# The first product of a four-layer graph network kernel: one plain slice, then three slices by seven products

## The chip, the cores and the metric

The kernel runs on one core of a Trainium2 chip. The metric is the device time of one execution in microseconds, as the median of several runs; lower is better. Everything is computed in fp32.

## What is computed

`x` holds 8 batches of 2048 nodes with 64 features, `adj` is a dense 2048 x 2048 matrix. Four layers follow each other, each of the form `x = layernorm(x + layer(x))`. The change touches layer 0 only:

```
# layer 0, K = 3: As = [I, A, 2 A A - I]
x_g = einsum('knm,bmc->bnkc', A_stack, x)        # x, A x, 2 A (A x) - x
w   = einsum('nd,dkio->nkio', embedding, weight)  # weights of each node
b   = einsum('nd,do->no', embedding, bias)
x   = layernorm(x + einsum('bnki,nkio->bno', x_g, w) + b)
```

Layer 1 has two products with A in a row, each followed by weights and a relu; layer 2 has one; layer 3 has two, for A x and 2 A (A x) - x. Their weights are 64 x 64 for all nodes.

## The kernel before

`x` is laid out as 16 tiles of 128 nodes by 512 columns (8 batches of 64), kept on chip in `xy`, which has two slots for each node tile: slot 0 is x, slot 1 takes a product. A product with `adj` is a 2048 x 2048 by 2048 x 512 multiplication. TensorE holds a 128 x 128 piece of x (two batches, one "pair" p of four) as stationary operand and streams a piece of `adj` past it, up to 512 columns. One source matmul in fp32 is two matmul instructions in the trace.

**The later products** (`product`, lines 189 to 330) use a scheme of seven multiplications in place of eight, at two levels: `adj` is cut into quarters, sums of quarters stand in `comb[q]` in HBM, and sums of x are formed on VectorE. The names of the seven at the outer level are A11, A12, A22, S1, S2, S3 and S4; at the inner level (`inner`, line 207), seven of eight blocks again, each sub-sum being an addition of 128 x 512.

**The first product** (lines 545 to 597, matmuls at L558) doesn't use the scheme, as the sums aren't there yet: it multiplies plainly and, while doing so, VectorE forms the sums of `adj` that the later products load. It runs over four slices `ns`; slice `ns` holds the node tiles ns, ns + 4, ns + 8, ns + 12 of the output, all inputs, as four chunks `j` of 1 MB (L146). The chunks live in a ring of four buffers, so chunk j of the next slice can only be loaded when TensorE and VectorE are done with chunk j of this one. A slice is 4 chunks x 4 pairs x 4 tiles = 64 source matmuls of 512 columns.

For each slice `prepare` (L465) makes on VectorE: the inner sums of A11, A12 and A22 (tag `C`, four buffers of 1 MB), and S1, S2, S4, S3 (tag `T`, three buffers of 1 MB), each with inner sums of its own. Every one is written to `comb` by DMAs that GpSimd issues (L478): 10 MB a slice. GpSimd's queue is in order, and so is SyncE's, which issues the loads.

At the end of a slice ACT copies the four PSUM banks to `hT` (L581; tags u2 and u3, one buffer each), a DMA writes `hT` to `t1T` in HBM, and a job `back` is queued that transposes `hT` back to nodes (L336, L337) into slot 1. Jobs wait in `pump`, which runs one step of one job after each group of four matmuls. `biases` (L539), 16 small matmuls, is such a job. In the last slice VectorE adds the biases `pb` to slot 0 and centres it (L573 to L576), one chunk after another.

`load_weights` is called after slice 0; its loads stand in SyncE's queue ahead of the chunks of slice 1. `sum_weights` turns the weights into the forms that are used, in slice 1.

The tile framework orders instructions for each engine; an instruction in `keep_in_program_order` isn't moved against others. After the first product, `product(1, ...)` starts with the inner products A11 and S1, before the feature work of layer 0 (L633 to L652), which adds onto slot 0.

Of the kernel before, what the change touches and what calls it, by code (L numbers as in the profile page):

```python
# [16 lines left out]
P = 128  # L17
# [75 lines left out]
def kernel(  # L93
# [311 lines left out]

    if True:
        l0 = first.enter_context(tc.tile_pool(name="l0", bufs=1))
        e_sb = l0.tile([P, NT, D], F32, tag="e_sb", name="e_sb")
        nc.gpsimd.dma_start(e_sb, emb)

        wn = l0.tile([P, 3, D, F], F32, tag="wn", name="wn")

        def center(w, half=slice(0, P)):
            shape = list(w.shape)
            m = small.tile([P, shape[1]], F32, tag="wm", name="wm")[half]
            nc.vector.tensor_reduce(m, w, AX.X, ALU.add)
            nc.vector.scalar_tensor_tensor(
                w, m.unsqueeze(2).to_broadcast(shape), -1.0 / F, w, ALU.mult, ALU.add
            )

        def load_weights():
            for k in range(2):
                nc.sync.dma_start(wn[k * F : (k + 1) * F], w_l0.rearrange("n i d o -> i n d o"))
            nc.gpsimd.memset(wd, 0.0)
            w3 = l0.tile([P, 5, F], F32, tag="s", name="w3", bufs=2)
            for k in range(2):
                half = slice(k * F, (k + 1) * F)
                for i, src in ((W1A, w_l1[0]), (W1B, w_l1[1]), (W2N, w_neigh), (W2S, w_self)):
                    nc.sync.dma_start(wd[half, i, half], src)
                nc.sync.dma_start(w3[half], w_l3.rearrange("(k i) o -> i k o", i=F))  # L430
            nc.sync.dma_start(b2, b_l2.to_broadcast([P, F]))
            nc.sync.dma_start(b3, b_l3.to_broadcast([P, F]))
            return w3

        def sum_weights(w3):
            nc.vector.tensor_tensor(wn[:, 0], wn[:, 0], wn[:, 2], ALU.subtract)
            nc.vector.tensor_scalar(wn[:, 2], wn[:, 2], 2.0, None, ALU.mult)

            for k in range(2):
                half = slice(k * F, (k + 1) * F)  # L440
                nc.vector.tensor_tensor(wd[half, W3A, half], w3[half, 1], w3[half, 3], ALU.add)
                nc.vector.tensor_tensor(w3[half, 2], w3[half, 2], w3[half, 4], ALU.add)
                nc.vector.tensor_tensor(wd[half, W3X, half], w3[half, 0], w3[half, 2], ALU.subtract)
                nc.vector.tensor_scalar(wd[half, W3AA, half], w3[half, 2], 2.0, None, ALU.mult)


            for k in range(2):
                half = slice(k * F, (k + 1) * F)
                center(wd[half, W2N:, half], half)
            for w in (W2S, W3X):  # L450
                nc.vector.tensor_tensor(wd[:, w, :], wd[:, w, :], ident, ALU.add)
            center(wn.rearrange("p n d o -> p (n d) o"))
            for k in range(2):
                half = slice(k * F, (k + 1) * F)
                for n, w in enumerate((W3A, W3X)):
                    nc.vector.tensor_copy(w3o[half, n], wd[half, w, half])
                for n, w in enumerate((W2N, W2S)):
                    nc.vector.tensor_copy(w2o[half, n], wd[half, w, half])
            center(b2.unsqueeze(1))
            center(b3.unsqueeze(1))  # L460

        def prepare(ns, ch):

            ch = [c.rearrange("p m i n -> p i m n") for c in ch]

            def add(out, a, b, op=ALU.add):
                nc.vector.tensor_tensor(out, a, b, op)

            def kept(tag, shape, bufs):
                s = sums.tile([P, *shape, GW], F32, tag=tag, name="s" + ("i" if tag == "C" else "o"), bufs=bufs)
# [25 lines left out]
            def rq(I, J):  # L498
                return lambda c: ch[2 * J + c][:, 2 * I : 2 * I + 2]
# [4 lines left out]
            def put(q, s):  # L504
# [2 lines left out]
                keep(q, 3, flat[:, 3:])  # L507
                inner(q, *(flat[:, k].rearrange("p (m n) -> p m n", m=TG) for k in range(4)))

            inner(A11, *raw(0, 0))  # L510
            inner(A12, *raw(0, 1))
            inner(A22, *raw(1, 1))
            s1 = outer(rq(1, 0), rq(1, 1), ALU.add)
            put(S1, s1)
            s2 = outer(sq(s1), rq(0, 0), ALU.subtract)
            put(S2, s2)
            s4 = outer(rq(0, 1), sq(s2), ALU.subtract)
            put(S4, s4)
            s3 = outer(rq(0, 0), rq(1, 0), ALU.subtract)
            put(S3, s3)  # L520

        with tc.tile_pool(name="p_n", bufs=4, space=PSUM) as p_n, tc.tile_pool(
            name="p_tn", bufs=2, space=PSUM
        ) as p_tn, tc.tile_pool(name="p_b", bufs=1, space=PSUM) as p_b:

            rise = p_tn.tile([P, TG, P], F32, tag="pt", name="rise")
            for k in range(8):
                nc.tensor.matmul(rise[:, k % TG, :], ident, ident, start=True, stop=True)

            bias0 = sums.tile([D, F], F32, tag="p1", name="bias0")  # L530
            nc.scalar.dma_start(bias0, b_l0)
            pb = p_b.tile([P, NT, F], F32, tag="pb", name="pb")
            eT = [l0.tile([D, GW], F32, tag="xT" if g < 2 else "tT", name="eT", bufs=2) for g in range(NG)]
            for g in range(NG):
                nc.scalar.dma_start(eT[g], embT[:, ts(g, GW)])

            def biases():
                for t in range(NT):
                    tc.keep_in_program_order(nc.tensor.matmul(  # L539
                        pb[:, t, :], eT[t // TG][:, ts(t % TG, P)], bias0, start=True, stop=True  # L540
                    ))
                    if t % TG == TG - 1:
                        yield

            for ns in range(TG):
                tiles = slice(ns, NT, TG)
                ps = [p_n.tile([P, GW], F32, tag="mm", name="ps_n") for p in range(NP)]
                ch = [chunks.pop((ns, j)) for j in range(NG)]
                prepare(ns, ch)
                if ns == 1:  # L550
                    sum_weights(w3)
                for j in range(NG):
                    steps = [(p, m) for p in range(NP) for m in range(TG)]
                    if ns == 0 and j == 0:

                        steps = [(p, m) for m in range(TG) for p in range(NP)]
                    for k, (p, m) in enumerate(steps):
# [5 lines left out]
                            stop=(j == NG - 1 and m == TG - 1),  # L563
                            skip_group_check=True,
                        )
                        if ns == j == k == 0:
                            tc.keep_in_program_order(mm)
                        if k % TG == TG - 1:
                            pump.step()
                    if ns == TG - 1:  # L570
                        v = xy[:, j * TG : (j + 1) * TG, 0, :].rearrange("p t (b f) -> p t b f", f=F)
                        bias = pb[:, j * TG : (j + 1) * TG, :].unsqueeze(2).to_broadcast([P, TG, B, F])
                        nc.vector.tensor_tensor(v, v, bias, ALU.add)  # L573
                        sm = small.tile([P, TG, B], F32, tag="xm", name="xm")
                        nc.vector.tensor_reduce(sm, v, AX.X, ALU.add)
                        nc.vector.scalar_tensor_tensor(  # L576
                            v, sm.unsqueeze(3).to_broadcast([P, TG, B, F]), -1.0 / F, v, ALU.mult, ALU.add
                        )
                for p in range(NP):
                    hT = sums.tile([P, GW], F32, tag=f"u{2 + p % 2}", name="hT")  # L580
                    nc.scalar.copy(hT, ps[p])  # L581
                    nc.sync.dma_start(
                        t1T[p].rearrange("f (i n c) -> f i n c", i=NG, n=TG)[:, :, ns],
                        hT.rearrange("f (i c) -> f i c", i=NG),
                    )

                    def back(p=p, hT=hT, tiles=tiles):
                        to_nodes(1, p_tn, tiles, p, hT)
                        yield
                    pump.add(back())  # L590
                if ns + 1 < TG:
                    for j in range(NG):
                        chunks[ns + 1, j] = slice_chunk(ns + 1, j)
                if ns == 0:
                    w3 = load_weights()
                    pump.add(biases())
            pump.drain()

        p_mm = ctx.enter_context(tc.tile_pool(name="p_mm", bufs=2, space=PSUM))
        if True:  # L600
            p_y = first.enter_context(tc.tile_pool(name="p_y", bufs=3, space=PSUM))


            order = [
# [5 lines left out]
            def fetch(k):  # L610
                if k < len(order):
                    i, p = order[k]
                    fetched[i, p] = [l0.tile([P, GW], F32, tag=n, name=n, bufs=2) for n in ("xT", "tT")]
                    for tile_, src in zip(fetched[i, p], (xT, t1T)):
                        nc.sync.dma_start(tile_, src[p][:, ts(i, GW)])

            def feature0(g, p, hT):
# [4 lines left out]
                for k in range(TG):  # L622
# [1 line left out]
                    acc = xy[:, t, 0, ts(p, 2 * F)].rearrange("p (b f) -> p b f", f=F)  # L624


                    s = l0.tile([P, DH, 2, F], F32, tag="s", name="s", bufs=2)
                    for h in range(2):
                        y = p_y.tile([P, 2, DH * F], F32, tag="y", name="y")
                        for n in range(3):  # L630
# [159 lines left out]
```

## Time and profile before

| | us |
|---|---|
| median of 3 runs (1723.04 to 1724.67) | 1723.25 |
| the profiled execution | 1724.72 |
| its span | 1722.9 |
| mean granted TensorE clock | 0.997 |
| first product: first matmul at | 6.05 |
| first product: end of its last matmuls at | 241.0 |

The busy shares of the engines in stretches of the first 250 us (us busy; the last two columns are the mean busy share of the 16 DMA engines and what they moved):

| stretch, us | TensorE | VectorE | ACT | DMA share | GB/s |
|---|---|---|---|---|---|
| 0 to 25 | 22.52 | 5.20 | 1.28 | 0.92 | 327 |
| 25 to 50 | 25.00 | 20.55 | 0.00 | 1.02 | 338 |
| 50 to 75 | 22.91 | 20.00 | 2.25 | 1.02 | 386 |
| 75 to 100 | 25.00 | 21.06 | 2.24 | 0.79 | 274 |
| 100 to 125 | 25.00 | 5.76 | 1.17 | 0.92 | 359 |
| 200 to 225 | 25.00 | 22.14 | 0.41 | 1.01 | 375 |

A busy share says how long an engine had something to do, not whether that was on the path that sets the end. The chain that ended last goes back from the last instruction through what released each one; its pieces, in order of time, show how long a run of instructions took from start to start. In a row of instructions the columns are line, engine, operation, output and inputs, shapes and count, busy time and mean duration in ns, and the idle time in front of it with what ended it. In a row of the windows they are the stretch, its length, busy us (and instructions) of TensorE, its weight loads, VectorE, ACT and GpSimd, the granted clock, the DMA share and GB/s.

### The profile page before, as it was taken

The numbers are of one execution on the slowest core, as the hardware profiler recorded it, in microseconds if no ns is written. First come the engines' busy times: TensorE is split into PE (matmuls) and PEld (weight loads), VectorE is DVE, ScalarE is ACT, GpSimd is POOL, SyncE is SP. The second block draws the span as 40 slices with busy tenths as digits, with TensorE's granted clock in tenths as the row PEclk, the third lists the DMA queues.
The fourth block names the chain that finished last, engine by engine and source line by source line (L and its number), as shares of the span: only waits on it lengthen the run. The fifth ranks groups of instructions, "written<-read, shape, count | busy, mean of one in ns | idle before, by whom it ended". The sixth has DMA issues, their size and how long they took to land.

```text
span 1722.9 us, 15569 instructions
## 1 busy us (share of the span) xinstructions
PE 1704.1 (99%) x5664; PEld 798.5 (46%) x5664; DVE 921.2 (53%) x1650; ACT 271.4 (16%) x772; POOL 258.5 (15%) x332
## 2 busy tenths in 40 slices
PE   9999999999999999999999999999999999999997
PEld 4444444444444444444455455554444455554443
DVE  4845773546546655544443264873557434443556
ACT  0100110232233333330001010221001012100001
POOL 1212200345245445441000000000000000000000
PEclk9999999999999999999999999999999999999999
DMA  9888768424422222227877877667888866678893
GB/s 325 331 324 317 253 233 302 149 86 138 167 86 99 86 99 86 98 74 291 314 273 268 296 279 250 221 221 258 294 294 285 302 229 214 225 263 301 316 314 123
DMA packets 82235, 391.19 MB, mean 227 GB/s; under 512 B 8848, under 2 KB 25232, under 8 KB 42608
## 3 DMA queue, kind: packets, MB, share of 16 engines
q1 hardware_dynamic: 70176, 346.94, 57.0%
q0 software_dynamic: 11248, 42.08, 6.7%
q10 hardware_dynamic: 736, 1.18, 0.2%
q8 instruction: 45, 0.74, 0.2%
q14 instruction: 30, 0.25, 0.0%
HBM read 339.84 MB, written 50.33 MB: 226 GB/s over the span
## 4 chain that ended last, share of the span: by engine, by line
PE 95%; DVE 3%; DMA 1%; ACT 0%; POOL 0%; issue 0%; POOLq 0%; ACTq 0%
PE mmb L225 25%; PE y L633 19%; PE mmc L225 16%; PE mma L225 16%; PE ps_n L558 12%; PE z L681 2%; PE z L711 2%; DMA t1T<-hT 1%; PE pt L672 1%; PE pt L727 1%; DVE ss L368 0%; PE pt_n L336 0%; DVE sm L352 0%; DVE xy L353 0%; DVE xy L378 0%; PE pb L539 0%
## 5 line engine op out<-in xcount | busy, mean ns | idle before, releaser
L225 PE MATMUL mmb<-a,t 128*128 128x512 f32 x1008 | 456.6, 595 | 0.0
L225 PEld LDWEIGHTS mmb<-a,t 128*128 128x128 f32 x1008 | 187.1, 190 | 227.2 <-issue 222.9
L641 DVE SCALAR_TENSOR_TENSOR xy<-y,e_sb,xy 128x128 f32<-128x128 f32 x512 | 179.7, 351 | 122.3 <-PE y L633 106.3
L558 PE MATMUL ps_n<-a,xy 128*128 128x512 f32 x512 | 225.5, 598 | 2.1 <-ACT hT L581 2.1
L650 POOL TENSOR_TENSOR s<-s 128x512 f32<-128x512 f32 (+2 forms) x192 | 167.0, 870 | 349.9 <-ACT s L645 339.9
L645 ACT ACTIVATE s<-y,e_sb 128x128 f32<-128x128 f32 x512 | 139.2, 383 | 293.1 <-PE y L633 293.1
L225 PE MATMUL mma<-a,T 128*128 128x512 f32 x384 | 173.5, 594 | 1.7 <-ACT p L240 1.7
L198 DVE TENSOR_TENSOR u<-mmb,p 128x512 f32<-128x512 f32 x84 | 58.0, 691 | 198.9 <-PE mmb L225 198.7
L225 PE MATMUL mmc<-a,t 128*128 128x512 f32 x336 | 152.4, 595 | 0.0
L558 PEld LDWEIGHTS ps_n<-a,xy 128*128 128x128 f32 x512 | 96.9, 192 | 118.5 <-issue 115.7
L633 PE MATMUL y<-wn,xT 64*128 64x512 f32 x512 | 135.6, 602 | 0.0
L633 PE MATMUL y<-wn,tT 64*128 64x512 f32 x512 | 132.1, 589 | 0.0
L225 PE MATMUL mma<-a,xy 128*128 128x512 f32 x288 | 130.5, 595 | 0.8 <-ACT hT L581 0.8
L633 PE MATMUL y<-wn,C 64*128 64x512 f32 x512 | 131.3, 589 | 0.0
L225 PEld LDWEIGHTS mma<-a,T 128*128 128x128 f32 x384 | 71.0, 190 | 87.1 <-issue 84.2
L198 DVE TENSOR_TENSOR C<-mmc,C 128x512 f32<-128x512 f32 x60 | 41.4, 690 | 109.5 <-PE mmc L225 109.5
L225 PEld LDWEIGHTS mmc<-a,t 128*128 128x128 f32 x336 | 61.5, 190 | 71.4 <-issue 71.0
L225 PE MATMUL mmc<-a,T 128*128 128x512 f32 x192 | 86.5, 593 | 0.0
L225 PEld LDWEIGHTS mma<-a,xy 128*128 128x128 f32 x288 | 53.5, 190 | 65.3 <-issue 61.2
L633 PEld LDWEIGHTS y<-wn,xT 64*128 64x128 f32 x512 | 47.1, 186 | 70.2 <-issue 70.2
L240 ACT COPY p<-mma 128x512 f32<-128x512 f32 x42 | 24.6, 586 | 343.3 <-PE mma L225 343.3
L633 PEld LDWEIGHTS y<-wn,tT 64*128 64x128 f32 x512 | 49.9, 187 | 60.3 <-issue 60.3
(97 smaller groups left out, 1340.7 us busy)
## 6 DMA issues: line engine op xcount, KB each, us to landing
a<-comb SPq DMA_DIRECT2D x240, 1024.0 KB, 4.8
a<-in_blocks SPq DMA_DIRECT2D x54, 1024.0 KB, 4.9
comb<-si POOLq DMA_DIRECT2D x28, 1024.0 KB, 10.0
a<-in_slices SPq DMA_DIRECT2D x15, 1024.0 KB, 9.8
comb<-so POOLq DMA_DIRECT2D x16, 512.0 KB, 11.4
comb<-so POOLq DMA_DIRECT2D x16, 256.0 KB, 11.8
t1T<-hT SPq DMA_DIRECT2D x16, 256.0 KB, 4.0
xT<-in_xT SPq DMA_DIRECT2D x16, 256.0 KB, 3.0
```

The lines of the kernel that those rows point to most:

```text
L198: nc.vector.tensor_tensor(out, a, b, op)
L225: nc.tensor.matmul(ps, xb[:, m, :], a[:, :, m, :], start=(start and m == 0), stop=(m == TG - 1), skip_group_check=True,)
L240: nc.scalar.copy(p1, pa)
L558: mm = nc.tensor.matmul(ps[p], xcol(0, TG * j + m, p), ch[j][:, m], start=(j == 0 and m == 0), stop=(j == NG - 1 and m == TG - 1), skip_gr ...
L633: nc.tensor.matmul(y[:, b, :], terms[n][half, ts(k, P)], wn[half, n, h * DH : (h + 1) * DH, :], start=(n == 0), stop=(n == 2),)
L641: nc.vector.scalar_tensor_tensor(acc, y[:, :, ts(d, F)], e, acc, ALU.mult, ALU.add)
L645: nc.scalar.activation(s[:, d], y[:, :, ts(d, F)], AF.Copy, scale=e)
L650: nc.gpsimd.tensor_tensor(s[:, :n], s[:, :n], s[:, n : 2 * n], ALU.add)
L672: nc.tensor.transpose(pt[:, ts(k, P)], xy[:, g * TG + k, slot, ts(p, 2 * F)], ident)
L681: nc.tensor.matmul(z[:, k, :], aT[:, ts(k, P)], wd[:, w, :], start=(n == 0), stop=(n == len(terms) - 1),)
L711: nc.tensor.matmul(z[n][:, k], xT[half, ts(k, P)], w[half], start=True, stop=True)
L727: nc.tensor.transpose(pt[:, k, :], hT[:, ts(k, P)], ident)
```

## The change

Slice 0 stays plain. Slices 1 to 3 use the scheme of seven at one level: S1 to S4 and the raw quarters of `adj` are streamed as they are made for `comb` (they lie on chip anyway), 256 columns at a time, past sums of x. Those sums, T1 to T4, are formed once on VectorE during slice 0; two of them lie in tiles of slot 1 that are written last (so slice 2's `back` jobs are held until slice 3 has used T1), two in a new pool `xs`. A slice becomes 7 products x 16 source matmuls of 256 columns. `prepare` is a generator now and forms the sums in another order, pinned from slice 1 on. Results are joined on VectorE (`plus`, `done`) rather than copied by ACT. `hT` has five buffers (tag `t`, which also takes `w3`); `w3` is loaded by ACT's queue. The biases are added in four pieces (`join_bias`), and centring is put into jobs that `product(1, ...)` runs during its first two inner products.

```diff
         def load_weights():
...
-            w3 = l0.tile([P, 5, F], F32, tag="s", name="w3", bufs=2)
+            w3 = sums.tile([P, 5, F], F32, tag="t", name="w3", bufs=5)
...
-                nc.sync.dma_start(w3[half], w_l3.rearrange("(k i) o -> i k o", i=F))
+                nc.scalar.dma_start(w3[half], w_l3.rearrange("(k i) o -> i k o", i=F))
...
-            inner(A11, *raw(0, 0))
-            inner(A12, *raw(0, 1))
-            inner(A22, *raw(1, 1))
-            s1 = outer(rq(1, 0), rq(1, 1), ALU.add)
-            put(S1, s1)
-            s2 = outer(sq(s1), rq(0, 0), ALU.subtract)
-            put(S2, s2)
-            s4 = outer(rq(0, 1), sq(s2), ALU.subtract)
-            put(S4, s4)
-            s3 = outer(rq(0, 0), rq(1, 0), ALU.subtract)
-            put(S3, s3)
+            outers[S1] = s1 = outer(rq(1, 0), rq(1, 1), ALU.add)
+            outers[S2] = s2 = outer(sq(s1), rq(0, 0), ALU.subtract)
+            inner(A11, *raw(0, 0))
+            outers[S3] = s3 = outer(rq(0, 0), rq(1, 0), ALU.subtract)
+            yield
+            put(S1, s1)
+            yield
+            put(S2, s2)
+            outers[S4] = s4 = outer(rq(0, 1), sq(s2), ALU.subtract)
+            inner(A12, *raw(0, 1))
+            inner(A22, *raw(1, 1))
+            yield
+            put(S3, s3)
+            put(S4, s4)
+            yield
...
+            def sums_of_x():
+                sub = ALU.subtract
+                nc.vector.tensor_tensor(T[0], xq(0, 1), xq(0, 0), sub)
+                nc.vector.tensor_tensor(T[1], xq(1, 1), T[0], sub)
+                nc.vector.tensor_tensor(T[2], xq(1, 1), xq(0, 1), sub)
+                nc.vector.tensor_tensor(T[3], xq(1, 0), T[1], sub)
...
+                def mul(ps, a, b, start=True):
+
+                    for p in range(2):
+                        for k in range(NT // 2):
+                            nc.tensor.matmul(
+                                ps[:, ts(p, GW // 2)], b(k, p), a(k // TG, k % TG),
+                                start=(start and p == k == 0), stop=(k == NT // 2 - 1),
+                                skip_group_check=True,
+                            )
+                        pump.step()
+                    return ps
...
+                next(parts)
+                pa = mul(bank(), raw(0, 0), x_of(0, 0))
+                p1 = sums.tile([P, GW], F32, tag="p1", name="p1")
+                nc.scalar.copy(p1, pa)
+                load_chunks(ns + 1, 0, 1)
+                next(parts)
+                p2 = mul(bank(), raw(0, 1), x_of(1, 0))
+                if ns == TG - 1:
+                    join_bias(0, 1)
+                    join_bias(0, 0)
+                pc = mul(bank(), summed(S1), t_of(1))
+                for job in held:
+                    pump.add(back(*job))
+                next(parts)
+                if ns == 1:
+                    sum_weights(w3)
+                elif ns == 2:
+                    sum_wn()
+                pb_ = mul(bank(), summed(S2), t_of(2))
+                u2 = plus("u2", pb_, p1)
+                done(0, p2, p1)
+                pd = mul(bank(), raw(1, 1), t_of(4))
+                load_chunks(ns + 1, 2, 3)
+                nc.vector.tensor_tensor(u2, pc, u2, ALU.add)
+                next(parts)
+                if ns == TG - 1:
+                    join_bias(1, 0)
+                mul(pb_, summed(S3), t_of(3), start=False)
+                u3 = plus("u3", pb_, p1)
+                done(3, pc, u3)
+                done(2, pd, u3)
+                pe = mul(bank(), summed(S4), x_of(1, 1))
+                done(1, pe, u2)
+                return [hT[p] for p in range(NP)]
...
+        def centered(h, c):
...
+            tc.keep_in_program_order(nc.vector.tensor_reduce(sm, v, AX.X, ALU.add))
+            yield
...
+                nc.vector.scalar_tensor_tensor(v, sm, -1.0 / F, v, ALU.mult, ALU.add)
+            )
+            yield
+
+        for h, c in ((0, 0), (0, 1), (1, 1), (1, 0)):
+            pump.add(centered(h, c))
```

`sum_wn` is the part of `sum_weights` that treats `wn`, in slice 2 now. `outer` writes a whole quarter sum, `put` writes it to `comb` and forms its inner sums, `done` adds a product half to a joined part into `hT`.

## Prediction

> **What bounds the kernel now.** I read the page's engine row first, then the chain that ended last, then the chain piece by piece for the first 250 us, which is all that the change touches.
>
> ```profile
> PE 1704.1 (99%) x5664; PEld 798.5 (46%) x5664; DVE 921.2 (53%) x1650; ACT 271.4 (16%) x772; POOL 258.5 (15%) x332
> ...
> PE 95%; DVE 3%; DMA 1%; ACT 0%; POOL 0%; issue 0%; POOLq 0%; ACTq 0%
> ...
> L558 PE MATMUL ps_n<-a,xy 128*128 128x512 f32 x512 | 225.5, 598 | 2.1 <-ACT hT L581 2.1
> ```
>
> TensorE is the chain: 95% of the span, and L558, the first product, is some 219 us of it. It idled there for 2.1 us in all, so time goes only if TensorE's stream shortens and nothing new makes it wait. A source matmul is two instructions in the trace (512 for 256 written).
>
> The pieces of the chain give the price of one instruction:
>
> ```profile
> 143.09 44.63 PE ps_n L558 x104
> ```
>
> 44.63 / 104 = 0.429 us for 512 columns; the mean of 598 ns in the group includes overlapped latency and isn't used. For narrow ones, TensorE's timeline in a later stage:
>
> ```profile
> 1002.35 1.05 PE L681 MATMUL z<-wd,C 128*128 128x128 f32 x8
> 1003.24 3.60 PE L225 MATMUL mmc<-a,t 128*128 128x512 f32 x8
> ```
>
> Eight instructions of 128 columns, each with its own weights, take 1003.24 - 1002.35 = 0.89 us, 0.111 us each. And the one stall, on the same timeline:
>
> ```profile
> 69.09 0.60 PE L336 MATMUL pt_n<-ident,hT 128*128 128x128 f32 x4
> 71.79 5.40 PE L558 MATMUL ps_n<-a,xy 128*128 128x512 f32 x8 [2.09 <-ACT hT L581]
> 77.02 0.60 PE L336 MATMUL pt_n<-ident,hT 128*128 128x128 f32 x4
> ```
>
> After 2.09 us of idling, eight instructions took 5.40 us against 3.43. The windows show why, and what the DMA engines did meanwhile:
>
> ```profile
> 60.00:64.00 4.00, 4.00 (x11) 1.77 (x10) 3.87 (x11) 0.00 (x0) 0.00 (x0) 1.00 1.01 416
> ...
> 72.00:76.00 4.00, 4.00 (x6) 1.62 (x6) 4.00 (x6) 1.23 (x3) 0.00 (x0) 0.57 0.99 336
> ...
> 80.00:84.00 4.00, 4.00 (x14) 2.00 (x13) 4.00 (x7) 0.59 (x1) 1.14 (x2) 1.00 0.08 30
> ```
>
> The granted clock (third from the end) fell to 0.57. The DMA share (next) is 1.0 in nearly every such window from 4 to 76 us: the first slice is DMA-bound in bytes although TensorE doesn't feel it. The waits name the stall's cause: hT has one buffer per tag and its previous copy to t1T was slow.
>
> ```profile
> ACT hT L581 <- DMA t1T<-hT: 18.2, 2, 15.4
> ```
>
> **Part by part.**
>
> *Matmuls.* Slices 1 to 3 held 384 instructions of 512 columns: 384 x 0.429 = 164.8 us. They become 3 x 7 products x 16 x 2 = 672 of 256 columns. No row has 256 columns; a line through 128 (0.111) and 512 (0.429) gives 0.217, so 672 x 0.217 = 145.9. Saved 18.9 us. Bounds: half of a 512 is 0.2146 (144.2 us, 1.7 more saved), 10 ns more each would cost 6.7. A rule of the Trainium skill speaks against the change (TensorE: Matmul & The Clock Gate, "Measured speedup vs the span model"): a weight load overlaps a running matmul only when it goes to another row group. Here all are 128 x 128, and this trace's weight loads last 190 ns. If they were exposed, an instruction would cost 0.213 + 0.190 = 0.403, 271 us, 106 us slower. But z's 0.111 us per instruction is shorter than one 190 ns load, so loads do overlap here; the row decides. Bias matmuls (4 x 1.03 us) and transposes (0.44 per four) keep their number.
>
> *hT buffers.* hT moves to five buffers of tag t, so ACT doesn't wait for t1T after slice 0. The stall goes: 2.1 idle plus 5.4 - 3.4 = 2.0 of slow clock, 4.1 us. The skill's advice (same page, "Why this matters for your kernels") is to avoid idling beyond about 3 us; by it a 2.09 us stall costs only itself. This row shows twice that, and I use the row. Next to be late there is slice 1's chunk 3, below.
>
> *VectorE.* Per fast slice: 28 inner additions at 0.60 spacing (17), 8 outer halves of 1.14 to 1.22 (9.5), u2, u3 and the second u2 addition (2.1), 8 half evictions, costed by the 128x256 addition from z at L716 (0.416, 3.3): 32 us, plus 8.6 for wn in slice 2 or 6.9 for three join_bias in slice 3, of some 50 us of TensorE. The order is pinned, so I laid both queues side by side. In slice 2, from its start: done(1) of slice 1 until 1, S1's sums 3.5, S2's 5.9, A11 and S3's 10.9, inner sums of S1 and S2 and done(0) 16.6; s4 waits for the third product, 22.5 (its buffer is S1's); A12 and A22 until 29.8; u2 at 33, needed by the accumulating S3 product at 36.2; u3 45.2, done(3) 46, needed at 50.2 by the next slice. All hide with 3 to 4 us in hand. Behind s4's wait stand A12, A22 and u2; u2 has the thinnest margin, 1 to 3 us in slice 1. Sums of x (4 x 2.28 = 9.1) fall into slice 0, where VectorE was busy 5.2 of the first 25 us: nothing, as slice 1 first needs them at 80.
>
> *Chunks.* Chunks 0 and 1 of the next slice can load once S3's sum and the first product are over, some 11 us into a slice, and have over 30 us. Chunks 2 and 3 load after the fifth product (36 us in), needed 21 us later; landing took 8.9 us in the median, 17.0 at most. Hidden, except in slice 1: there chunk 3 needs the buffer that slice 0 uses to its end, and the fast slice reads it in its second product.
>
> ```profile
> 61.98 0.33 SPq L146 DMA_DIRECT2D a<-in_slices  x1
> ```
>
> ```profile
> 79.01 1.29 DVE L469 TENSOR_TENSOR si<-a 128x512 f32<-128x512 f32 x2 [2.93 <-DMA a<-in_slices]
> ```
>
> The first row is SP's timeline, the second VectorE's. In before it was issued at 61.98 and was there at 79.0, behind three other chunks issued at 48 to 51 and the t1T writes. Slice 0 ends at 62.0, so TensorE needs it at 62.0 + 2 x 3.47 + two bias groups of 1.03 + half a group, 1.7, = 72.7. SP's queue is the weights, then chunks 0, 1, 2, three t1T writes, then chunk 3. Without two w3 loads in it, and with S3's sum early on VectorE, chunks 0 and 1 go at some 41 instead of 48; chunk 2 at some 55 (VectorE waits in slice 0 for S1's write to free s4's buffer). From 48 to 79 this queue moved about 5 MB, 155 GB/s, beside the saturated writes. From 55.5: chunk 2, 0.75 MB of t1T, chunk 3, 2.75 MB / 155 GB/s = 17.7, so 73.2. Wait 0.5 us; the bounds are 0 and 79.0 - 72.7 = 6.3 plus 2 of slow clock. I take 2.5, nearer to the queue sum than to before's landing, with some for the clock and u2.
>
> *w3* moves to ACT's queue behind the hT copies: issued about 62, landing in 9.2 (median before), so 71 to 72, and slice 1's weight sums stand on VectorE between the halves of S1's sum. S1's product is at 80, the sum at 75 to 77: nothing, up to 3 if w3 takes 15.
>
> *Biases and end of stage.* Three join_bias (2.29 each) hide as above; the last follows the stage's end, 2.3 us before the new product's first difference. Until now bias and reduction (4.6) stood there. The first two transposes no longer wait for ACT's hT copies (0.8 idle). Together nothing, -1 to +1.
>
> *Deferred centring.* Eight operations of 2.29 = 18.3 us enter the first two inner products of product 1 (16 groups of 3.43 = 55 us), where VectorE is busy some 20 now by its timeline. A u addition must come within one group (3.43) after its product; one centring operation plus the addition is 3.0. The long differences (2.28) added once make 0.3. I take 0.4, 0 to 4; without cover, 18.3. From product 1's feature work onward every engine's order is unchanged.
>
> **Sum.** 18.9 + 4.1 - 2.5 - 0.4 = 20.1 us. The profiled run is 1724.7 (span 1722.9, 1.8 around it), giving 1704.6; it lies 1.5 over the median of 1723.25, so the median to expect is 1703.2, say 1703.5.
>
> **Rivals.**
> - *Chunk 3 of slice 1 as late as before.* It speaks for this that the DMA engines are full until 76 us in any order, and that the sums of slice 0 end some us later. Then 8.5 instead of 2.5: 1709.5. Against it: SP's queue drains earlier.
> - *Writes of sums hold VectorE in slices 2 and 3.* 15 MB per slice in 50 us is 300 GB/s; saturated windows moved 340 to 420. If C buffers come free late, VectorE slips past its 3 to 4 us of margin, 3 to 5 us per slice with slow clock: about 1713.
> - *Slower: exposed weight loads.* Place: each of 672 instructions. Gain and loss balance at (164.8 + 4.1 - 2.9) / 672 = 0.247 us, so from 34 of the 190 ns exposed. With 48 exposed, 0.261 x 672 = 175.4: 10.6 lost, 4.1 won, 2.9 of waits, so 1733. Against it: z at 0.111.
> - *That it doesn't do what it says* is excluded: the built order has 336 source matmuls of 256 columns (672 instructions) and 64 of 512.
>
> **Numbers.** Forecast 72% (its own range 1700 to 1707), late chunk 15%, writes 7%, exposed loads 3%, other losses 3%. Low end 1700: no waits and 0.2146 per instruction would be 1698.7, which needs all at once. High end 1710.5 takes in the late chunk. A difference under about 0.2% (3.4 us) can't be told from none. Faster 0.94, same 0.02, slower 0.04.
>
> **What would show it.** 256-column instructions at 0.214 to 0.22 spacing in the chain; no clock loss near 70 us, or a short wait for in_slices at about 72 at the first fast slice's second product; the stage ending near 221 instead of 241; product 1's first 55 us with VectorE full but TensorE at 4.00 of 4.00. I am wrong if the spacing is over 0.23, if waits recur in slices 2 and 3, or if u additions wait for centring.

## The result, and the profile after

The changed kernel takes 1704.0 us (median of 4 runs, 1703.34 to 1711.45) beside 1723.96 for the kernel before on the same chip (4 runs, 1723.04 to 1725.07): a ratio of 0.9894, 95% interval 0.9866 to 0.9922. The profiled execution took 1703.86 us, its span is 1702.1 (before on that chip: 1724.72 and 1722.9), and the mean granted clock is 0.997 in both. The forecast was 1703.5. One execution of the runs below, the profiled one of the first hT run, took 6417.3 us and counts in no figure.

The page of the changed kernel, its engine row and the chain by engine:

```profile
PE 1684.3 (99%) x5952; PEld 853.6 (50%) x5952; DVE 941.9 (55%) x1687; ACT 266.9 (16%) x763; POOL 258.3 (15%) x332
...
PE 96%; DVE 3%; DMA 1%; ACT 0%; POOL 0%; issue 0%; POOLq 0%
```

TensorE is 19.8 us less busy with 288 more instructions, and still is the chain. A DMA has 1% of it, as before, but it is another one: before it was t1T<-hT ahead of the hT stall (18.74 us from 52.30). The chain in order of time says what a 256-column instruction costs, where the first product ends, and which DMA it is now (start us, us, what):

```profile
61.77 13.62 DMA a<-in_slices
...
136.82 58.71 PE ps_n L653 x272
...
221.46 0.89 PE pt_n L336 x8
```

58.71 / 272 = 0.2158 us per instruction, and the stage's matmuls end at 221.46, where the forecast had 0.214 to 0.22 and near 221. But the chain hangs on one load for 13.62 us, of which TensorE sat out a part. Its timeline there:

```profile
70.83 1.99 PE L653 MATMUL ps_n<-a,xy 128*128 128x256 f32 x8
75.43 3.40 PE L653 MATMUL ps_n<-a,xy 128*128 128x256 f32 x8 [2.60 <-DMA a<-in_slices]
78.75 1.33 PE L553 MATMUL pb<-bias,eT 16*128 16x64 f32 x8
80.02 3.72 PE L653 MATMUL ps_n<-a,xy 128*128 128x256 f32 x16
```

Eight instructions from 70.83 are over at 70.83 + 8 x 0.2158 = 72.56; the next start at 75.43, 2.87 us later. They then need 3.40 us where 1.73 is normal, and the bias group behind them 80.02 - 78.75 = 1.27 where 1.03 is normal. 2.87 + 1.67 + 0.24 = 4.8 us in all. The windows show the clock and the DMA engines:

```profile
68.00:72.00 4.00, 4.00 (x22) 3.33 (x21) 0.00 (x0) 0.59 (x1) 0.00 (x0) 1.00 0.94 305
72.00:76.00 4.00, 1.40 (x6) 0.90 (x5) 1.56 (x8) 0.00 (x0) 0.00 (x0) 0.98 0.52 170
76.00:80.00 4.00, 4.00 (x15) 2.88 (x13) 4.00 (x5) 0.00 (x0) 1.28 (x2) 0.59 0.23 89
```

The clock fell to 0.59 after the wait, as it had fallen to 0.57 after the hT stall before. The DMA share is still 0.94 from 68 to 72 and falls from 73 on; chunk 3 lands at 75.4, among the last of what was under way. SyncE's timeline gives its issue, and VectorE's the landing of w3 (`w`):

```profile
38.85 9.51 SPq L146 DMA_DIRECT2D a<-in_slices  x3
...
61.77 0.33 SPq L146 DMA_DIRECT2D a<-in_slices  x1
```

```profile
72.83 0.22 DVE L443 TENSOR_TENSOR wd<-w 64x64 f32<-64x64 f32 x1 [12.10 <-DMA w<-in_w_l]
...
75.57 0.22 DVE L443 TENSOR_TENSOR wd<-w 64x64 f32<-64x64 f32 x1 [1.52 <-DMA w<-in_w_l]
...
76.37 1.21 DVE L471 TENSOR_TENSOR so<-a 128x1024 f32<-128x1024 f32 x1
```

The other three chunks left early, as foreseen; chunk 3 left at 61.77, when slice 0 had freed its buffer, and landed 13.6 us later. Over the whole stage TensorE waited for nothing else after its start, not once in slices 2 and 3 (its waits from 0 to 260 us):

```profile
PE ps_n L653 <- DMA a<-in_slices: 2.6, 1, 2.6
PE rise L539 <- POOL ident masks.py:199: 2.1, 1, 2.1
```

### The profile page after: what moved, and what is told of

It is laid out like the page before. It is cut to its first block, busy times and chain, and to the rows that moved or that the text cites. A ratio compares the mean times of both kernels' runs of the same rounds, so it can differ in the third digit from the quotient of the medians.

```text
span 1702.1 us, 16167 instructions
## 1 busy us (share of the span) xinstructions
PE 1684.3 (99%) x5952; PEld 853.6 (50%) x5952; DVE 941.9 (55%) x1687; ACT 266.9 (16%) x763; POOL 258.3 (15%) x332
## 4 chain that ended last, share of the span: by engine, by line
PE 96%; DVE 3%; DMA 1%; ACT 0%; POOL 0%; issue 0%; POOLq 0%
PE mmb L225 25%; PE y L790 20%; PE mmc L225 17%; PE mma L225 16%; PE ps_n L653 8%; PE ps_n L616 3%; PE z L838 2%; PE z L868 2%; PE pt L829 1%; DMA a<-in_slices 1%; PE pt L884 1%; PE pt_n L336 0%; DVE ss L368 0%; DVE sm L352 0%; DVE xy L353 0%; DVE xy L378 0%
## 5 line engine op out<-in xcount | busy, mean ns | idle before, releaser
L790 PEld LDWEIGHTS y<-wn,C 64*128 64x128 f32 x512 | 49.6, 187 | 60.3 <-issue 60.1
L225 PE MATMUL mmc<-a,xy 128*128 128x512 f32 x144 | 65.1, 594 | 0.0
```

Source lines behind the costliest of these rows:

```text
L225: nc.tensor.matmul(ps, xb[:, m, :], a[:, :, m, :], start=(start and m == 0), stop=(m == TG - 1), skip_group_check=True,)
L790: nc.tensor.matmul(y[:, b, :], terms[n][half, ts(k, P)], wn[half, n, h * DH : (h + 1) * DH, :], start=(n == 0), stop=(n == 2),)
```

## Experiments

My theory: narrower matmuls give 19.8 us, the stall for hT gives 4 to 5, and a wait for chunk 3 of slice 1 takes back 5 to 7, since that chunk queues behind everything that the DMA engines still have to move. The rivals: the matmuls aren't at their floor because of weight loads; VectorE's work or the centring costs part of what is missing. There are three groups of runs, each with its own runs of the kernel before on the same chip (medians 1724.99, 1725.09, 1724.88), so differences are taken within a group.

**The hT stall alone**: the kernel before with one edit.

```diff
-                    hT = sums.tile([P, GW], F32, tag=f"u{2 + p % 2}", name="hT")
+                    hT = sums.tile([P, GW], F32, tag="t", name="hT", bufs=5)
```

> The kernel before with hT in tag t with five buffers, and nothing else changed. My theory: the hT buffers are worth the stall and the slow clock after it, 2.1 + 2.0 = 4.1 us, so about 1719.8 and a granted clock of 1.00 near 72 us. Rival: the DMA engines are full there anyway, another wait takes its place, and the time stays within 1 us of 1723.9.

1720.24 us beside 1724.99: ratio 0.9973 (0.9964 to 0.9983), 4.75 less. The same kernel once more, for its profile:

> The kernel before with hT in tag t with five buffers once more, as the profiled execution of its first run was disturbed and shows nothing. First run: 4.7 us under the kernel before. My theory: no idle time at L558 behind an hT copy, granted clock 1.00 between 68 and 80 us, and chunk 3 of slice 1, still landing near 79, waited for by VectorE alone; about 4.5 us under the kernel before.

1720.11 beside 1724.88, ratio 0.9973 (0.9963 to 0.9984), 4.77 less. TensorE's timeline of this run, at the place of the stall:

```profile
73.06 3.60 PE L558 MATMUL ps_n<-a,xy 128*128 128x512 f32 x8
76.50 0.60 PE L336 MATMUL pt_n<-ident,hT 128*128 128x128 f32 x4
```

No wait, and eight instructions in 76.50 - 73.06 = 3.44 us. The buffers were worth 4.8 us by two measurements, where the rows of the stall had given 4.1. A second wait is gone in this trace too: in the kernel before TensorE waited 0.77 us for an hT copy at the end of the stage (ahead of product 1's instructions at 242.63), which would cover the difference. The buffers alone are a quarter of the change's gain.

**Are the fast matmuls held by weight loads?** Each is split into two of 128 columns, with the same sum of columns and twice the weight loads.

```diff
-                            nc.tensor.matmul(
-                                ps[:, ts(p, GW // 2)], b(k, p), a(k // TG, k % TG),
+                            for h in range(2):
+                                nc.tensor.matmul(
+                                    ps[:, ts(2 * p + h, P)], b(k, p), a(k // TG, k % TG)[:, h],
...
```

> The changed kernel with every matmul of the fast slices cut into two of 128 columns, so twice as many weight loads (1344) for the same sums. If weight loads lie beside matmuls: 1344 x 0.111 = 149.2 against 145.1, 4 us slower than the changed kernel, about 1708. Rival (part of each 190 ns load is exposed, and already at 256): the exposed part grows with the count, at least 30 us slower.

1706.04 beside 1724.99, ratio 0.9894 (0.9880 to 0.9909). The long piece of its chain:

```profile
136.26 60.75 PE ps_n L654 x544
```

60.75 / 544 = 0.1117 us. 1344 x 0.1117 = 150.1 against 672 x 0.2158 = 145.0: 5.1 us more for 672 more instructions, 8 ns each. A weight load takes about 190 ns in these traces; were it exposed, 672 more would have cost over 100 us. That rival is out. This run also showed something else, in its timeline and its windows:

```profile
70.03 2.05 PE L654 MATMUL ps_n<-a,xy 128*128 128x128 f32 x16
74.67 2.05 PE L654 MATMUL ps_n<-a,xy 128*128 128x128 f32 x16 [2.58 <-DMA a<-in_slices]
```

```profile
76.00:78.00 2.00, 2.00 (x17) 1.81 (x16) 2.00 (x2) 0.00 (x0) 1.28 (x2) 1.00 0.25 96
```

The wait for chunk 3 is as long as in the changed kernel (2.58 and 2.60), but the clock stayed at 1.00. In time this run is 19.0 us below its runs of the kernel before, the changed kernel 20.0 in its first result and 18.3 in the next run; such scatter hides the 4 us that were expected.

**The changed kernel again**, in the third group.

> The changed kernel as it is, on the same chip as the version with both remedies. The runs that let the chunk come in time gained 6 to 7 us where the profile of the changed kernel shows 4.8 of wait and slow clock. My theory: the wait for chunk 3 varies from run to run (landing 13.6 to 16 us after the issue in four profiles), so single times spread over 1700 to 1710, with a median 20 us under the kernel before. Rival: the spread was the other kernels'; the changed kernel stays within 1 us.

1706.63 (1704.15 to 1709.87) beside 1724.88, ratio 0.9895 (0.9877 to 0.9913). The profiled execution was the slowest of the four, 1709.87, and shows why:

```profile
70.58 1.99 PE L653 MATMUL ps_n<-a,xy 128*128 128x256 f32 x8
77.40 3.78 PE L653 MATMUL ps_n<-a,xy 128*128 128x256 f32 x8 [4.83 <-DMA a<-in_slices]
81.11 1.97 PE L553 MATMUL pb<-bias,eT 16*128 16x64 f32 x8
83.01 6.67 PE L653 MATMUL ps_n<-a,xy 128*128 128x256 f32 x16
```

```profile
76.00:78.00 2.00, 0.60 (x2) 0.51 (x3) 0.94 (x4) 0.00 (x0) 0.00 (x0) 0.50 0.15 51
...
88.00:90.00 2.00, 2.00 (x10) 1.46 (x8) 1.97 (x5) 0.00 (x0) 0.34 (x1) 0.75 1.02 260
```

A gap of 77.40 - 72.31 = 5.1 us, and then half speed until 89: eight instructions in 3.71 us (1.73 normal), a bias group in 1.90 (1.03), sixteen in 6.60 (3.65), 5.8 lost. Together 10.9 us, 6.1 more than in the first profile, and its span is 5.9 longer. So between these two executions the scatter is this wait and its clock. Of the other six there is no trace, but their mean granted clocks agree: 0.997 in the four executions from 1703.3 to 1704.2, 0.994 in those of 1709.87 and 1711.45 (of the latter, 1.7 us lie outside its span of 1707.9).

**Chunk 3 from another place**: the load goes into tiles of slot 1 that are free, so it needn't wait for slice 0's buffer.

```diff
-                    load_chunks(1, *range(NG))
+                    load_chunks(1, *range(NG - 1))
+                    a = xy[:, 1:NT:TG, 1, :].rearrange("p t (i n) -> p t i n", i=NG)
+                    nc.sync.dma_start(a, slices[1, NG - 1])
+                    chunks[1, NG - 1] = a
```

> The changed kernel with chunk 3 of slice 1 loaded into four tiles of slot 1 that are written only in slice 2, so it needn't wait for the end of slice 0 (issue at about 48 instead of 61.8). My theory: it lands by 65 to 68, the wait at 72.6 and the slow clock go, 4.8 us; next late is w3 (landed 72.8 and 75.6), behind which the second half of S1's sum stands, and S1's product is due at 79.7: no wait. About 24.8 us under the kernel before, 1699. Rival: the DMA engines are full until 75 whatever the order, so w3 or S1's sum is late instead and 1703 stays.

1698.32 (1698.06 to 1698.65) beside 1725.09: ratio 0.9841 (0.9826 to 0.9857), 26.8 less, faster than both kernels. SyncE's timeline, then TensorE's, then a window:

```profile
40.05 0.99 SPq L146 DMA_DIRECT2D a<-in_slices  x2
41.49 0.59 SPq L723 DMA_DIRECT2D xy<-in_slices  x1
```

```profile
70.28 1.99 PE L653 MATMUL ps_n<-a,xy 128*128 128x256 f32 x8
72.11 1.89 PE L653 MATMUL ps_n<-xy 128*128 128x256 f32 x8
73.93 1.10 PE L553 MATMUL pb<-bias,eT 16*128 16x64 f32 x8
74.96 1.99 PE L653 MATMUL ps_n<-a,xy 128*128 128x256 f32 x8
```

```profile
72.00:76.00 4.00, 4.00 (x23) 3.32 (x22) 3.96 (x7) 0.00 (x0) 0.96 (x2) 1.00 1.05 389
```

Issued 20 us earlier, the chunk is there when it is read (the second row, from xy), the clock stays at 1.00, and the stage ends at 216.41, 5.05 earlier. About 0.5 of that lies ahead of the wait, in slice 0; the same pieces took 74.96 - 70.28 = 4.68 us here and 80.02 - 70.83 = 9.19 in the changed kernel, so the wait cost 4.5 by this count, beside 4.8 by the one above. The DMA engines are fuller than in the changed kernel (1.05 here, 0.52 there, from 72 to 76): what counted was the chunk's place in the order, not how full the engines were.

**Less to move ahead of chunk 3.** wn's loads, 1.6 MB, stood in SyncE's queue ahead of slice 1's chunks although they are needed in slice 2. First they were put behind those chunks:

```diff
-            for k in range(2):
-                nc.sync.dma_start(wn[k * F : (k + 1) * F], ...)
...
                     load_chunks(1, *range(NG))
+                    load_wn()
```

> The changed kernel with the two wn loads (1.5 MB in small packets) issued after the chunks of slice 1 instead of ahead of them. My theory: chunk 3 of slice 1 is late because the DMA engines are full, so 1.5 MB less in front lets it land 4 us earlier or more, before 72.6; its wait and the slow clock after it (2.9 + 1.9 = 4.8 us) go, about 1699.2. Rival: chunk 3 is late because of the order in its own queue (chunk 2 waits for VectorE); then it lands 1 us earlier at most and 1703 stays.

1705.73 beside 1724.99, ratio 0.9890 (0.9876 to 0.9905). SyncE's timeline shows that the edit didn't do what it says:

```profile
31.36 0.36 SPq L146 DMA_DIRECT2D a<-in_slices  x1
31.77 2.54 SPq L433 DMA_DIRECT2D wn<-in_w_l  x2
```

The scheduler put them behind the first chunk only, 29 us ahead of chunk 3 (60.77). Inconclusive. The second try ties them to slice 1 by a copy that needs u2, and gives them to ACT's queue (they are taken out of `load_weights` as above):

```diff
+        def load_wn(u):
+            tc.keep_in_program_order(nc.vector.tensor_copy(wn[:, 0, 0, :1], u[:, :1]))
+            for k in range(2):
+                nc.scalar.dma_start(wn[k * F : (k + 1) * F], ...)
...
                 u2 = plus("u2", pb_, p1)
+                if ns == 1:
+                    load_wn(u2)
```

> The changed kernel with the two wn loads (1.5 MB) issued by ACT only after slice 1's u2, at about 102 us, instead of at 15 us; one VectorE copy of one column orders them. In the run with wn after the chunks in program order, the loads still went out at 32 us, ahead of chunk 3, and nothing was tested. My theory: chunk 3 lands when all that was issued before it has drained, so 1.5 MB less at some 400 GB/s brings it 3.7 us earlier, to about 71.7, before it is needed at 72.6: the wait and the slow clock go, 4.8 us, so about 24.8 us under the kernel before. Rival: the landing follows chunk 3's own queue and the number of buffers for sums (VectorE waits for writes of sums in slice 0 anyway); then it lands within 1 us of 75.4.

1698.96 (1698.56 to 1699.98) beside 1725.09, ratio 0.9846 (0.9830 to 0.9861), 26.1 less. Its windows:

```profile
68.00:72.00 4.00, 4.00 (x23) 3.32 (x22) 0.19 (x2) 0.58 (x1) 0.00 (x0) 1.00 0.63 192
72.00:76.00 4.00, 4.00 (x22) 3.32 (x21) 3.87 (x10) 0.00 (x0) 0.63 (x1) 1.00 0.02 6
```

Chunk 3 is issued at 61.51, nearly as late as in the changed kernel, but it lands 9.8 us later instead of 13.6, the DMA engines are drained by 72 (0.02 after it), and TensorE doesn't wait. That is the theory from its other side: less ahead of it, nearly the same issue time, an earlier landing. What was less is seen on VectorE, first in the changed kernel, then in this run:

```profile
51.50 1.29 DVE L471 TENSOR_TENSOR si<-so 128x512 f32<-128x512 f32 x2 [3.77 <-DMA comb<-si]
...
56.49 0.69 DVE L471 TENSOR_TENSOR si<-so 128x512 f32<-128x512 f32 x1 [3.09 <-DMA comb<-si]
```

```profile
49.23 0.69 DVE L474 TENSOR_TENSOR si<-so 128x512 f32<-128x512 f32 x1 [0.42 <-DMA comb<-si]
```

In the changed kernel VectorE waits 6.9 us in slice 0 for the writes of its own sums to free their buffers, so GpSimd issues the last three writes ahead of chunk 3 at 58.1 to 59.9; here at 50.8 to 52.6. From chunk 3's issue to its landing 2.50 MB of such writes moved in the changed kernel, and 0.68 MB here.

**Both at once**:

> The changed kernel with both: chunk 3 of slice 1 in slot 1, and the wn loads after slice 1's u2. My theory: nothing is left to gain once TensorE waits for no chunk in slice 1, so the time is that of either alone, 1698 to 1699, with a spread under 1 us. Rival: the fuller DMA queues still cost something in one of them; then the two together are over 1 us faster than the better one.

1698.99 beside 1724.88, ratio 0.9850 (0.9835 to 0.9864). No more than either alone: once the wait is gone, making it go twice buys nothing.

**Later need**: slice 1's bias groups all go into its first product (`rate=2` for that product), so that chunk 3 is read 2 us later.

```diff
...
-                        pump.step()
+                        pump.step(rate)
...
-                pa = mul(bank(), raw(0, 0), x_of(0, 0))
+                pa = mul(bank(), raw(0, 0), x_of(0, 0), rate=2 if ns == 1 else 1)
```

> The changed kernel with all four groups of bias matmuls put between the halves of slice 1's first product, so the second product comes 2 x 1.03 us later with no more work. My theory: the wait for chunk 3 shrinks from 2.9 to 0.8 us and the clock is not lowered any more: 2.1 + 1.9 = 4.0 us gained, about 1700. If the loss of clock comes with any wait at all: 2.1 gained, 1702. Rival (the wait isn't decided by when the chunk lands): no gain.

1702.62 beside 1724.99, ratio 0.9868 (0.9852 to 0.9885), 22.4 less; the changed kernel was 20.0 and 18.3 below its runs of before. So 2.4 to 4.1 us come back. The wait was expected to shrink to 0.8 us; it is 3.08, as chunk 3 landed at 76.6 here, 15.9 us after its issue, and the clock fell again (1.8 us lost):

```profile
76.66 3.50 PE L653 MATMUL ps_n<-a,xy 128*128 128x256 f32 x8 [3.08 <-DMA a<-in_slices]
```

**Centring left out** (the jobs aren't queued).

```diff
-        for h, c in ((0, 0), (0, 1), (1, 1), (1, 0)):
-            pump.add(centered(h, c))
```

> The changed kernel without the centring of slot 0 ahead of layer 0's feature work (eight VectorE operations left out, so x isn't centred before the feature sums are added). My theory: TensorE never waits for them, so the time stays within 0.4 us of the changed kernel (about 19.9 to 20.4 us under the kernel before). Rival: centring is part of what the stage pays; if its 18.3 us were half exposed, 9 us faster.

1704.76 (1700.68 to 1709.82) beside 1725.09, ratio 0.9877 (0.9847 to 0.9907): the scatter hides anything small in the time. The chain tells more, from the first mmb in its place to the long run of y:

```profile
230.47 3.43 PE mmb L225 x8
...
289.23 9.64 PE y L788 x44
```

58.76 us. In the changed kernel the same pieces start at 229.01 and 287.77, 58.76 as well. Deferred centring costs 0.00 us of TensorE's time there.

**VectorE's margin**: four reductions of 2.28 us, whose results nothing uses, around u2 in slice 2 (on VectorE from 152.8 to 163.4).

```diff
+                    for n in range(EXTRA):
...
+                        tc.keep_in_program_order(nc.vector.tensor_reduce(sm, v, AX.X, ALU.add))
```

> The changed kernel with four more reductions of 2.28 us on VectorE in slice 2, results unused. The trace after shows u3 of slice 2 ready about 4 us before the bank that it frees is needed. My theory: 9.1 us more eat that margin and cost 9.1 - 4.3 = 4.8 us plus some 2 of slow clock, so 5 to 7 us slower than the changed kernel. Rival (VectorE isn't near the path there): no change; the opposite rival (no margin at all): 9 us or more.

1707.87 beside 1725.09, ratio 0.9894 (0.9877 to 0.9912), within the changed kernel's scatter. TensorE's timeline at the end of slice 2:

```profile
172.85 0.60 PE L337 MATMUL pt_n<-ident,hT 128*128 128x128 f32 x4
174.75 14.08 PE L654 MATMUL ps_n<-a,xy 128*128 128x256 f32 x64 [1.30 <-DVE u L676]
```

Some 8.8 us of added work cost a wait of 1.3 us, without a loss of clock (1.00 from 172 to 178). The expectation, 5 to 7 us, missed by its size, for two reasons. TensorE waits there for the addition u3 only, and the two that follow it are off the path: in the changed kernel u3 ends at 166.2 and the next product begins at 171.2, a margin of 5.0 us and not 4.3. And three inner sums (0.60 each) that stood ahead of u3 stand behind it here, so that u3 comes only 6.9 us later. Of the 1.9 us by which that exceeds the margin, 0.44 went into four transposes ahead of the wait.

## Why the prediction was right, and where a size was off

1. *Matmuls.* 0.217 was read off a line through 128 and 512 columns; 0.2158 was measured. 164.8 - 145.0 = 19.8 instead of 18.9. The bound of exposed weight loads is refuted by the split into 128 columns. (Its 0.213 stands in no row; with the 0.217 of the line it would have been 109 us instead of 106.) The rule that the prediction set against the row stands in the Trainium skill under "The mechanism" of the page it names (TensorE: Matmul & The Clock Gate); that section lets a load into the background weight buffer be pulled ahead as well. Here the loads were hidden at 256 and at 128 columns, so the rule alone doesn't describe this kernel; which buffer they went to no run shows.
2. *hT stall.* Foreseen 4.1, measured 4.8 twice with the buffers alone, in which the wait of 0.77 us at the end of the stage is included.
3. *Chunk 3 of slice 1: the term that was mis-sized.* The step was "2.75 MB / 155 GB/s = 17.7, so 73.2. ... I take 2.5". The place, the need (72.7; 72.56 measured) and the kind of wait were right. It landed at 75.4, and the term measured 4.8 in this profile, 10.9 in the second. Two things were sized wrongly. I counted one queue, SyncE's, at a rate taken from before, with chunk 2 in it from 55.5. But chunk 2 had left at 48.0 and landed at 56.1, and chunk 3 was still later: from its issue to its landing SyncE's queue moved 1.74 MB, 128 GB/s instead of 155 (in the trace of before it was 5.24 MB from 48 to 79, which is 169), while GpSimd's writes took 2.50 MB. Over all queues it was 322 GB/s x 13.4 = 4.3 MB between 62.0 and 75.4 while this 1 MB landed. Then the clock: the same kind of wait lost 0 us of clock (the 128-column run), 1.9 (first profile) or 5.8 (second). "2 of slow clock" stood in the bounds and had nearly no weight in the value taken. The rival of a late chunk, 1709.5, described the slower executions of this very kernel (1709.87, 1711.45); the forecast described the faster ones.
4. *w3.* Foreseen at 71 to 72; its two halves came at 72.8 and 75.6, and S1's sum ended behind them, at some 77.6. S1's product was at 84.7, itself pushed back by the wait for chunk 3, so it cost nothing. With chunk 3 early S1's product came at 79.6, and TensorE didn't wait there either.
5. *VectorE in slices 2 and 3.* No wait of TensorE, as foreseen. In slice 2 the first u2 addition, which reads the bank, ends at 152.9, and the product that accumulates onto that bank begins at 157.4: 4.5 us in hand; u3 has 5.0. The rival of full write queues is out for these slices. In slice 0 the writes did hold VectorE, for the 6.9 us above; in the run in which wn waits that hold is nearly gone, and chunk 3 comes in time.
6. *Boundary and centring.* Foreseen -1 to +1, and 0.4. From the stage's end to the first long run of y (9.64 us for 44 instructions, 0.219 each) it took 287.77 - 221.46 = 66.31 us after and 309.18 - 240.99 = 68.19 before; in before four more y instructions stood inside that stretch, 0.9, so about 1.0 us was saved, 0.77 of it the wait for an hT copy. Centring was 0.0.

The sum by this profile: -19.8 - 4.1 + 4.8 - 1.0 and 0.2 for an earlier end of slice 0 (61.77 instead of 61.98), -20.3; the spans differ by 20.8, and 0.5 isn't attributed (0.2 if the wait is counted as 4.5). The forecast's -20.1 came close because matmuls, boundary, slice 0 and centring gave 2.5 more than foreseen and the wait took 2.3 more. That these two cancelled is luck. So is a part of the 0.5 us between forecast and median: four of the eight executions of this kernel lie at 1703.3 to 1704.2, the others at 1706.2 to 1711.5, and the second median is 1706.6.

With the wait gone the kernel is at 1698.3 to 1699.0 by three ways, with 0.6 to 1.4 us between its fastest and slowest run in each, against 5.7 and 8.1 with it. TensorE then waits for nothing in this stage after its start; what else could shorten the stage wasn't tried.

## What to carry to other kernels

When a stage gets faster, look for the load whose issue is tied to a buffer that the stage before releases last; here its issue stayed where it was (61.98 before, 61.77 after), while TensorE needed it earlier. Its landing was decided here by the bytes that all queues still had to move, not by its own queue alone. Giving it another place, or shifting bytes that weren't due behind it, was worth 6 to 8 us here, and both together no more than either. Count a wait of TensorE with its clock, as a range: for waits of 2.1 to 5.0 us the clock took between 0 and 5.8 us more.

## What was not expected of the hardware

The clock's loss after a wait was not a function of its length here. Waits of TensorE by the profile, and what the instructions behind them took too long: 1.30 us (four reductions, in slice 2) and 0; 2.09 (hT, before) and 2.0; 2.58 (128 columns) and 0; 2.60 and 1.9; 3.08 and 1.8; 4.27 (wn behind the chunks) and 5.1; 4.70 (no centring) and 2.2; 4.83 and 5.8; 5.00 (four reductions) and 2.1. The losses stand in three groups, about 0, 2 and 5 to 6, and in the slow stretches the granted clock is 0.50: two is a stretch of some 4 us at half speed, 5.8 one of 11.6. The Trainium skill (TensorE: Matmul & The Clock Gate, "What's actually happening") says that the clock is halved after an idle window of about 3.4 us, and that these windows run freely. Losses in steps, and 0 or 1.9 for waits of one length, agree with a window that doesn't start with the wait. That a whole window has to be idle doesn't agree: waits of 2.09, 2.60 and 3.08 us are shorter than one, and the clock fell after each. Its advice (same page, "Why this matters for your kernels") to avoid gaps of more than about 3 us is too wide here: waits of 2.09 and 2.60 us lowered the clock. Why the clock came back after some 4 us in some runs and after 11 in two others stays open; no experiment set the phase of a wait.
